# A sparse two-layer graph network: row variances and neighbour scores on ScalarE, Newton steps an iteration later, the last tiles' rows added singly, the stairs behind the projections

## The chip, the cores and the metric

The kernel runs on one core of a Trainium2 chip. A core has five engines that work side by side, each with a queue of its own that it works off in order: TensorE (PE, with its weight loads as PEld), VectorE (DVE), ScalarE (ACT), GpSimd (POOL) and SyncE (SP). Transfers between the chip's memory (DRAM) and the core's SBUF are done by 16 DMA engines; they are issued from the queues of SP, ACT or POOL. The metric is the time of one execution on the device in microseconds (us), lower is better.

## What is computed

x has 3327 rows of 512 numbers, adj is a sparse 0/1 matrix of 3327 by 3327 with ones on the diagonal. Two layers follow one another, each with a residual and a layer norm. In short:

```python
def layer0(X, A, W, b, a_self, a_neigh):           # 4 heads of 128
    feats  = einsum('nf,hfo->hno', X, W)
    logits = leaky(e_s[:, :, None] + e_n[:, None, :], 0.2)   # e_s, e_n: feats . a_self, feats . a_neigh
    attn   = softmax(logits - 1e10 * (1 - A))
    return relu(concat_heads(attn @ feats) + b)

def layer1(x, A, W_sa, a_sa, W_g, b_g, Wa, ba, Wb, bb):
    gate_a = sigmoid([A @ x, x] @ Wa.T + ba)       # one number a row
    gate_b = sigmoid([A @ x, x] @ Wb.T + bb)
    h      = x @ W_sa
    e      = where(A, exp(-leaky(s_left[:, None] + s_right[None, :], 0.01)), 0)
    x_a    = (e / (e.sum(1) + 1e-5)) @ h
    x_b    = A @ (x @ W_g) + b_g
    return sigmoid(gate_a * x_a + gate_b * x_b)

x = layernorm(x + layer0(x, adj, ...))
x = layernorm(x + layer1(x, adj, ...))
```

A row has few neighbours, so the kernel doesn't multiply by A: it finds for each row the list of its neighbours, and gathers their rows.

## The kernel before

**Tiles.** The 3328 padded rows are 26 tiles of 128, in two groups of 12 and 14. Within a group the rows are sorted by their number of neighbours, so that a tile j needs only `CAPS[j]` gathered rows for each of its own (14 down to 4). The first tile of each group (0 and 12) holds the few rows with more neighbours; what they have beyond `CAPS` comes by an extra gather, the **stairs**: `to_row`, `to_node` and `step_of` are small matrices that spread these extra entries onto rows of a tile and back. `climb` works out which rows the stairs gather (`ids2`) and their own scores (`es2`): two VectorE copies out of the sorted lists `srt`, a matmul with `to_row`, and four small VectorE operations.

**Stage 1.** For each tile, `features` (line 338 on) multiplies x by W on TensorE (16 matmul records at L346), copies the result with ACT into a `row` of 512 features and 8 scores (L350, L351), and POOL writes it into a table in DRAM, `table0` (L353). After the last tile, POOL also writes a very negative score into the table's one padding row, from `nrow` (L355). Between the projections, seven chunks of 512 columns of adj are turned into lists of neighbours: `make_codes` (matmuls on loads `at` that SP issues, 12 buffers for 13 loads a chunk), `turn_codes` (transposes, `pv`), and then `top_codes`, `decode` and `pick` on VectorE. A `rank` and a scatter through DRAM sort the rows (`sort`; lists are read back as `srt`), and POOL gathers the sorted x (`own_x`, L496). The loop that orders this by hand is:

```python
    for i in range(len(chunks)):
        make_codes(i)
        more(1)                      # features of one tile
        ...
        turn_codes(i); top_codes(i); decode(i); pick(i)
        ...
        if i == NC0 + 1:
            climb(0, ...)
        more(4)                      # features of up to four tiles
```

NC0 is 3, so `climb` for the first group stands in chunk 4, ahead of the last `more(4)`, which has the last two tiles left to project.

**Stage 2, layer 0.** POOL gathers rows one indirect DMA at a time (L602, 128 rows of 520 numbers each), three tiles ahead, into 7 buffers of 6 rows. For tile i the loop does in this order: gather for tile i+3; `publish` tiles whose statistics are finished (ACT scales and shifts the row, VectorE the 8 columns beside it, POOL scatters it into `table1`); `columns2` of tile i-2 (ACT copies the transposed rows out of PSUM, L757, TensorE multiplies them by 8 vectors, L760); `attend` tile i (two of three gathered rows are multiplied by their weights on VectorE, L733, the third on ACT, L731, and TensorE adds all of them up through an identity matrix, L736); tile i-1's residual y (L810), its transposes (`columns1`, L753) and its statistics (`norm.add`); `columns3` (L764); and the weights of tile i+1, with an exponential on ACT (`weigh_a`, L696 to L709, and `weigh_b`, L714 to L716).

**The norm.** `Norm.add` takes bn_stats and bn_aggr of each y on VectorE (L647, L648). When a group of up to four tiles is full, `rsqrt` follows at once: 13 small VectorE operations (L656 to L663), the core of them three Newton steps.

**Stage 3, layer 1.** The same gathers, from `table1`. `weights_a` adds the row's own score to the neighbours' on VectorE (L863), takes leaky (L870), the exponential on ACT (L872) and the gates; `weights_b` divides. `weighted` sums the rows times e on VectorE (L930), and for up to four or five pairs of rows (`paired`) also adds the two rows of a pair (L932), so that TensorE, which sums the rows unweighted (`plain_sum`, L951), has one matmul instead of two. `turn` and `project` transpose and multiply both sums by W_sa and W_g (L961, L970); then come the gated sum (L995), a tanh (L997), the residual (L1018), the norm and the scatter of the result (L1011, L143). The tiles' order in this layer is short ones first, then long and short in turn; the last four are 3, 17, 18 and 8, with 10, 9, 9 and 7 rows.

Of the kernel before, what the change touches and what calls it, by code (L numbers as in the profile page):

```python
# [8 lines left out]
F32 = mybir.dt.float32  # L9
AF = mybir.ActivationFunctionType  # L10
ALU = mybir.AluOpType
# [68 lines left out]
def sparse_pass(  # L80
# [212 lines left out]
    nc.gpsimd.dma_start(table1[N:NP, :], zrow)  # L293
    nrow = pj.tile([1, ROW], F32, name="nrow")
    nc.gpsimd.memset(nrow, 0.0)
    nc.gpsimd.memset(nrow[:, F : F + H], -BIG)

# [41 lines left out]
    def features(t):  # L339

        i = t * P // CH
        xc = xcs[i]
        o = t * P - chunks[i]
        pf = psf.tile([P, 2, 512], F32, tag="pf", name=f"pf{t}")
        for k, hh in ((k, hh) for hh in range(2) for k in range(KT)):
            nc.tensor.matmul(  # L346
                pf[:, hh, :HC], xc[:, k, o : o + P], w0[:, k, hh, :], start=(k == 0), stop=(k == KT - 1)
            )
        row = pj.tile([P, ROW], F32, tag="row", name=f"row{t}", bufs=4)
        nc.scalar.copy(row[:, 0:F].rearrange("p (h o) -> p h o", h=2), pf[:, :, 0 : F // 2])  # L350
        nc.scalar.copy(row[:, F:ROW].rearrange("p (h o) -> p h o", h=2), pf[:, :, F // 2 : HC])  # L351
        nc.scalar.copy(st[:, t, S + 2 : S + 2 + H].bitcast(F32), pf[:, 1, F // 2 : HC])  # L352
        nc.gpsimd.dma_start(table0[t * P : (t + 1) * P, :], row)  # L353
        if t == NT - 1:
            nc.gpsimd.dma_start(table0[N:NP, F : F + H], nrow[:, F : F + H])  # L355

# [193 lines left out]
    for i in range(len(chunks)):  # L550
# [9 lines left out]
        if i == NC0 - 1:  # L560
            rank_a(0)
        if i == NC0 + 1:
            climb(0, p0, psl.tile([P, CH], F32, tag="pc1", name="climb0")[:, : B + H])
        more(4)
    later(len(tasks))
    nc.sync.dma_start(own1[:, 0, :], xo)
    nc.sync.dma_start(own1[:, 1, :], table0[NG[0] * P : NP, :])
    rank_a(1)
    rankis[1] = rank_b(1)
# [74 lines left out]

    def stats(pool, y, mv):
        st6 = pool.tile([P, 6], F32, tag="st6", name=f"st6_{nc.next_id()}")
        nc.vector.bn_stats(st6, y)  # L647
        nc.vector.bn_aggr(mv, st6)  # L648

    def rsqrt(pool, mv, n, tag):  # L650

        v = pool.tile([P, GRP], F32, tag="rv", name=f"rv{tag}")[:, :n]
        r = pool.tile([P, GRP], F32, tag="rr", name=f"rr{tag}")[:, :n]
        t = pool.tile([P, GRP], F32, tag="rt", name=f"rt{tag}")[:, :n]
        d = pool.tile([P, GRP], F32, tag="rd", name=f"rd{tag}")[:, :n]
        nc.vector.tensor_scalar(v, mv[:, :n, 1], LN_EPS, None, ALU.add)  # L656
        nc.vector.tensor_scalar(t.bitcast(I32), v.bitcast(I32), 1, None, ALU.logical_shift_right)
        nc.vector.tensor_scalar(r.bitcast(I32), t.bitcast(I32), -1.0, float(0x5F3759DF), ALU.mult, ALU.add)
        for _ in range(3):
            nc.vector.tensor_mul(t, r, r)  # L660
            nc.vector.scalar_tensor_tensor(t, t, -0.5, v, ALU.mult, ALU.mult)
            nc.vector.scalar_tensor_tensor(r, t, 1.5, r, ALU.add, ALU.mult)
        nc.vector.scalar_tensor_tensor(d, mv[:, :n, 0], -1.0, r, ALU.mult, ALU.mult)  # L663
        return r, d

    class Norm:


        def __init__(self, pool, tag, ends):
            self.pool, self.tag, self.ends = pool, tag, ends  # L670
            self.first, self.mv = 0, None

        def add(self, k, y):

            if self.mv is None:
                self.mv = self.pool.tile([P, GRP, 2], F32, tag="mv", name=f"mv{self.tag}{k}")
            stats(self.pool, y, self.mv[:, k - self.first, :])
            if k not in self.ends:
                return None
            n = k - self.first + 1  # L680
            done = (self.first, *rsqrt(self.pool, self.mv, n, f"{self.tag}{k}"))
            self.first, self.mv = k + 1, None
            return done
# [66 lines left out]
    def columns1(j):  # L750
        pt = turned[j] = psx.tile([P, KT, P], F32, tag="pt", name=f"x1t{j}", bufs=2)
        for k in range(KT):
            nc.tensor.transpose(pt[:, k, :], row1(j)[:, k * P : (k + 1) * P], ident)  # L753

    def columns2(j):
        xt1 = m0.tile([P, KT, P], F32, tag="xt1", name=f"xt1_{j}")
        nc.scalar.copy(xt1, turned[j])  # L757
        pcol = psx.tile([P, B * H], F32, tag="pcol", name=f"pcol{j}", bufs=2)[:, :NCOL]
# [34 lines left out]
    weigh_b(order0[0])  # L793
    ready = [[], []]
    for i in range(NT + 3):
        if i + AHEAD < NT:
            j = order0[i + AHEAD]
            got[j] = gather(table0, j)
        for args in ready[0]:
            publish(*args)  # L800
        ready = [ready[1], []]
        if 2 <= i < NT + 2:
            columns2(order0[i - 2])
        if i < NT:
            attend(order0[i])
        if 0 < i <= NT:
            j = order0[i - 1]
            y = row1(j)[:, 0:F]
            xj = y if j < NG[0] else got[j][0][2][:, 0, 0:F]
            nc.vector.scalar_tensor_tensor(y, accs[j], 0.0, xj, ALU.max, ALU.add)  # L810
            columns1(j)
            done = norm.add(i - 1, y)
            if done:
                k0, scale, shift = done
                ready[1] = [
                    (order0[k], scale[:, k - k0 : k - k0 + 1], shift[:, k - k0 : k - k0 + 1]) for k in range(k0, i)
                ]
        if 2 <= i < NT + 2:
# [37 lines left out]
    def weights_a(j):  # L856

        c = slots(j)
        e = ew[j] = m1.tile([P, S + 1], F32, tag="e", name=f"e{j}", bufs=3)
        gate = gates[j] = m1.tile([P, 12], F32, tag="gate", name=f"gate{j}", bufs=5)  # L860
        nc.scalar.copy(e[:, 0:1], row1(j)[:, F + 6 : F + 7])
        for s0, n, g, _ in got[j]:
            nc.vector.tensor_scalar(e[:, s0 : s0 + n], g[:, :n, F], row1(j)[:, F + 3 : F + 4], None, ALU.add)  # L863
        if j in T0:
            small = ps1.tile([P, B * H], F32, tag="small", name=f"to_nodes1_{j}")
            cols = to_nodes(m1, small, f"l1_{j}", stair[j][:, F : F + 3])
            nc.vector.scalar_tensor_tensor(
                e[:, C0 + 1 :], cols[:, :, 0], row1(j)[:, F + 3 : F + 4], no_step, ALU.add, ALU.subtract
            )
# [30 lines left out]
    def paired(j):  # L900

        left = 4 + (CAPS[j] >= 13)
        got_ = set()
# [68 lines left out]
    ends = {3, 7, 11, 15, 19, 22, 24, 25}  # L972
    norm = Norm(m1, "n1", ends)
    at_ = lambda i: order[i] if 0 <= i < NT else None
# [4 lines left out]
    scaled_first(at_(0))  # L979
    ready = None  # L980
    for i in range(NT + 3):
# [11 lines left out]
        if jpp is not None:  # L993
            za = zs[jpp] = m1.tile([P, F], F32, tag="za", name=f"za{jpp}", bufs=GRP + 3)
            nc.vector.scalar_tensor_tensor(za, bias_g, gates[jpp][:, 1:2], proj[jpp], ALU.mult, ALU.add)  # L995

            nc.scalar.activation(za, za, AF.Tanh, scale=0.5)  # L997
        if jp is not None:
            project(jp, 0)
# [16 lines left out]
        if jpp is not None:  # L1016
            za = zs[jpp]
            nc.vector.scalar_tensor_tensor(za, za, 0.5, row1(jpp)[:, 0:F], ALU.mult, ALU.add)  # L1018
        if j1 is not None:
            weights_b(j1)  # L1020
            scaled_first(j1)
        if jpp is not None:
            ready = norm.add(i - 2, zs[jpp])

# [451 lines left out]
```

## Time and profile before

| what | value |
|---|---|
| time, three runs | 1015.5, 1017.0, 1017.8 us |
| the profiled run | 1008.2 us, span 1006.5 us |
| PE busy | 798.0 us, 79% |
| DVE busy | 719.3 us, 71% |
| POOL busy | 635.8 us, 63% |
| ACT busy | 270.5 us, 27% |
| DMA | 221.9 MB, 220 GB/s on average |

A profile is one execution. Busy times are sums over the engine's own instructions, so an engine that waits for another shows as idle; the time between two instructions of a queue ("issue") isn't counted as busy either. The stages lie one behind the other: up to about 197 us projections and lists, to 593 us layer 0, then layer 1. Since their limits differ, an engine's share of the whole span says little: one asks in each stage which wait ends last.

### The profile page before, as it was taken

What the parts mean: (1) busy time and instruction counts of PE and PEld (TensorE: products, weight loads), DVE (VectorE), ACT (ScalarE), POOL (GpSimd) and SP (SyncE); (2) the same over time, 40 slices, a digit from 0 to 9 for tenths busy, and PEclk for the clock granted to TensorE, in tenths of its full rate; (3) what the DMA queues carried; (4) which work ended last, traced back from release to release, by engine and by line L of the source; (5) the groups of instructions that cost most, each with busy time, mean ns of one, the idle gap of its engine ahead of it and who ended that gap; (6) DMA issues with size and microseconds to landing.
All of it is one profiled execution on the core that took longest, in us unless ns stands there. A gap on an engine that the chain in (4) does not pass through costs nothing.

```text
span 1006.5 us, 9964 instructions
## 1 busy us (share of the span) xinstructions
PE 798.0 (79%) x2534; PEld 422.2 (42%) x2534; DVE 719.3 (71%) x2131; ACT 270.5 (27%) x737; POOL 635.8 (63%) x677
## 2 busy tenths in 40 slices
PE   4398982518797996989698949998998989898991
PEld 3277762204344443444344424444444434343440
DVE  4277896586366673856566848897987989899882
ACT  1021210103134242333424413323221232321331
POOL 6611151577777777777777647777777777777211
PEclk9699995657889998889899968999999999999996
DMA  8799995995877777777777537776776667767200
GB/s 321 291 356 400 367 388 197 322 372 200 269 206 206 219 207 225 209 232 229 218 237 230 178 118 199 192 193 197 192 194 194 177 185 189 199 184 190 72 32 34
DMA packets 71954, 221.86 MB, mean 220 GB/s; under 512 B 13425, under 2 KB 17697, under 8 KB 70993
## 3 DMA queue, kind: packets, MB, share of 16 engines
q0 software_dynamic: 48000, 157.07, 52.7%
q1 hardware_dynamic: 22784, 61.97, 16.3%
q10 hardware_dynamic: 1104, 2.10, 0.6%
q8 instruction: 23, 0.38, 0.1%
q14 instruction: 43, 0.34, 0.1%
HBM read 200.01 MB, written 28.54 MB: 227 GB/s over the span
## 4 chain that ended last, share of the span: by engine, by line
PE 31%; DMA 17%; POOL 17%; DVE 16%; issue 13%; ACT 4%; DVEq 0%; POOLq 0%; ACTq 0%
POOL g L602 12%; PE acc L736 12%; DMA g<-table,srt 12%; PE pf L346 8%; DVE sw L930 6%; PE po L970 3%; DVE g L932 2%; PE pcol L760 2%; DMA at<-in_adjB 2%; PE acc L725 2%; PE acc L951 2%; ACT za L1011 1%; POOL out L143 1%; DMA a_row<-in_a_self 1%; POOL sprod L316 1%
## 5 line engine op out<-in xcount | busy, mean ns | idle before, releaser
L602 POOL DMA_INDIRECT g<-table,srt x464 | 477.2, 1028 | 145.8 <-issue 126.0
L736 PE MATMUL acc<-g,ident 128*128 128x512 f32 x504 | 232.5, 618 | 1.5 <-DVE g L733 1.5
L930 DVE SCALAR_TENSOR_TENSOR sw<-g,e,sw 128x512 f32<-128x512 f32 x226 | 169.3, 749 | 15.8 <-ACT sw L914 11.7
L736 PEld LDWEIGHTS acc<-g,ident 128*128 128x128 f32 x504 | 101.2, 201 | 133.6 <-issue 105.9
L951 PE MATMUL acc<-g,ident 128*128 128x512 f32 x262 | 124.9, 606 | 19.7 <-DVE g L932 19.6
L346 PE MATMUL pf<-w,xc 128*128 128x260 f32 x416 | 100.1, 402 | 13.8 <-DVE w L289 13.8
L733 DVE TENSOR_TENSOR g<-g,w 128x512 f32<-128x512 f32 x176 | 110.5, 695 | 0.6
L970 PE MATMUL po<-wsa,sT 128*128 128x512 f32 x208 | 95.6, 603 | 0.2 <-ACT sT L963 0.2
L346 PEld LDWEIGHTS pf<-w,xc 128*128 128x128 f32 x416 | 82.5, 201 | 28.6 <-DVE w L289 14.3
L970 PE MATMUL po<-wg,sT 128*128 128x512 f32 x208 | 93.5, 593 | 0.0
L731 ACT ACTIVATE g<-g,w 128x128 f32<-128x128 f32 x304 | 91.6, 390 | 2.7 <-DVE w L716 2.7
L951 PEld LDWEIGHTS acc<-g,ident 128*128 128x128 f32 x262 | 49.1, 192 | 88.4 <-issue 44.2
L353 POOL DMA_DIRECT2D table<-row x26 | 14.4, 554 | 95.2 <-ACT st L352 81.2
L932 DVE TENSOR_TENSOR g<-g 128x512 f32<-128x512 f32 x95 | 65.7, 691 | 3.3
L696 DVE TENSOR_TENSOR w<-g,srt 128x20 f32<-128x20 f32 (+3 forms) x55 | 9.7, 180 | 80.7 <-DMA g<-table,srt 79.7
L760 PE MATMUL pcol<-v,xt 128*128 128x8 f32 x208 | 33.2, 287 | 40.5 <-ACT xt L757 40.5
L143 POOL DMA_INDIRECT out<-za,srt x26 | 28.3, 1090 | 54.7 <-ACT za L1011 48.6
L970 PEld LDWEIGHTS po<-wsa,sT 128*128 128x128 f32 x208 | 40.6, 195 | 51.7 <-issue 49.5
L997 ACT ACTIVATE za<-za 128x512 f32<-128x512 f32 x26 | 16.4, 632 | 167.0 <-DVE za L995 167.0
L970 PEld LDWEIGHTS po<-wg,sT 128*128 128x128 f32 x208 | 39.6, 190 | 49.7 <-issue 49.2
L709 ACT ACTIVATE w<-w 128x40 f32<-128x40 f32 (+10 forms) x26 | 6.2, 237 | 176.8 <-DVE w L708 176.8
L760 PEld LDWEIGHTS pcol<-v,xt 128*128 128x128 f32 x208 | 30.9, 228 | 46.0 <-ACT xt L757 46.0
(234 smaller groups left out, 954.5 us busy)
## 6 DMA issues: line engine op xcount, KB each, us to landing
at<-in_adjB SPq DMA_DIRECT2D x78, 512.0 KB, 11.7
g<-table,srt POOLq DMA_INDIRECT x464, 3.8
table<-row POOLq DMA_DIRECT2D x26, 260.0 KB, 5.8
xc<-in_xB SPq DMA_DIRECT2D x6, 1024.0 KB, 7.4
own<-in_xo SPq DMA_DIRECT2D x1, 3640.0 KB, 31.2
own<-table SPq DMA_DIRECT2D x1, 3640.0 KB, 49.6
at<-in_adjL SPq DMA_DIRECT2D x13, 256.0 KB, 7.3
w<-in_W0B SPq DMA_DIRECT2D x1, 1040.0 KB, 6.9
```

Of the source, the lines that this page charges most:

```text
L143: put = nc.gpsimd.indirect_dma_start(out=dst, out_offset=bass.IndirectOffsetOnAxis(ap=rows, axis=0), in_=src, in_offset=None, bounds_check ...
L346: nc.tensor.matmul(pf[:, hh, :HC], xc[:, k, o : o + P], w0[:, k, hh, :], start=(k == 0), stop=(k == KT - 1))
L602: nc.gpsimd.indirect_dma_start(out=buf[:, q - q0, :], out_offset=None, in_=table[:, :], in_offset=bass.IndirectOffsetOnAxis(ap=srt[g][:, i ...
L725: nc.tensor.matmul(acc, ident, bias0, start=True, stop=False)
L731: nc.scalar.activation(gv[:, h, :], gv[:, h, :], AF.Copy, scale=w[:, s, h : h + 1])
L733: nc.vector.tensor_tensor(gv, gv, w[:, s, :].rearrange("p (h o) -> p h o", o=1).to_broadcast([P, H, FO]), ALU.mult)
L736: nc.tensor.matmul(acc, ident, buf[:, o + s - s0, 0:F], start=False, stop=(s == CAPS[j] and j not in T0))
L760: nc.tensor.matmul(pcol, xt1[:, k, :], v1[:, k, :], start=(k == 0), stop=(k == KT - 1))
L930: nc.vector.scalar_tensor_tensor(sw, g[:, i, 0:F], e[:, s : s + 1], sw, ALU.mult, ALU.add)
L932: nc.vector.tensor_add(g[:, i, 0:F], g[:, i - 1, 0:F], g[:, i, 0:F])
L951: nc.tensor.matmul(plain[j], to, row, start=(not sums_of_two and i == 0), stop=(sums_of_two and i == len(rows) - 1),)
L970: nc.tensor.matmul(proj[j], sT[:, k, :], wt[:, k, :], start=(half + k == 0), stop=(half + k == KT))
```

## The change

1. **Variances.** bn_stats and bn_aggr go. The VectorE operation that makes y (L810, and L1018 in layer 1) also puts out its row sum; one small VectorE operation makes minus the mean of it, and ACT squares y with that as its bias and puts out the sum of squares (`AF.Square` with `accum_out`).
2. **Newton steps.** `rsqrt` becomes `Norm.finish` and is called one iteration after the group's last `add`: in layer 0 behind `attend`, in layer 1 behind the tanh. The published tiles and the iteration that uses the result stay.
3. **Scores.** In layer 1 the sums of scores (L863) are made by ACT (`AF.Identity` with a bias).
4. **Columns.** In layer 0 the copy out of PSUM moves from the head of `columns2` to the end of `columns1`, so one iteration's part of ACT's queue now has it ahead of the exponential of the next tile, and `columns2` itself comes behind `attend`.
5. **Unpaired rows.** For the last four tiles of layer 1 at most one pair of rows is added up on VectorE.
6. **Stairs.** `climb(0, ...)` moves from chunk 4 to behind the loop over the chunks, ahead of the second group's ranks.
7. **Padding row.** Its score isn't written by a DMA of its own; ACT's copy of the last tile's scores has a bias `pad` that is very negative in that row. `nrow` and its transfer go.

```diff
+    pad = p0.tile([P, 1], F32, name="pad")
+    nc.gpsimd.memset(pad, 0.0)
+    nc.gpsimd.affine_select(pad, pad, ..., fill=-BIG, base=P - 2, channel_multiplier=-1)
...
-        nc.scalar.copy(row[:, F:ROW]..., pf[:, :, F // 2 : HC])
+        nc.scalar.activation(row[:, F:ROW]..., pf[:, :, F // 2 : HC], AF.Identity,
+            bias=pad if t == NT - 1 else 0.0)
...
-        if t == NT - 1:
-            nc.gpsimd.dma_start(table0[N:NP, F : F + H], nrow[:, F : F + H])
...
-        if i == NC0 + 1:
-            climb(0, p0, psl.tile(...)[:, : B + H])
         more(4)
     later(len(tasks))
     nc.sync.dma_start(own1[:, 0, :], xo)
     nc.sync.dma_start(own1[:, 1, :], table0[NG[0] * P : NP, :])
+    climb(0, p0, psl.tile(...)[:, : B + H])
     rank_a(1)
...
-    def stats(pool, y, mv):
-        nc.vector.bn_stats(st6, y)
-        nc.vector.bn_aggr(mv, st6)
...
         def add(self, k, y):
+            nc.vector.tensor_scalar(less_mean, less_mean, -1.0 / F, None, ALU.mult)
+            nc.scalar.activation(square, y, AF.Square, bias=less_mean, accum_out=self.of[:, 1, i : i + 1])
+            return k in self.ends
+        def finish(self, k):               # what rsqrt did
...
     def columns1(j):
         ...
             nc.tensor.transpose(pt[:, k, :], row1(j)[:, k * P : (k + 1) * P], ident)
+        xt1s[j] = m0.tile([P, KT, P], F32, tag="xt1", name=f"xt1_{j}")
+        nc.scalar.copy(xt1s[j], pt)
     def columns2(j):
-        nc.scalar.copy(xt1, turned[j])
...
+        if i < NT:
+            attend(order0[i])
         if 2 <= i < NT + 2:
             columns2(order0[i - 2])
-        if i < NT:
-            attend(order0[i])
+        if full:
+            k0, scale, shift = norm.finish(i - 2)
...
-            nc.vector.scalar_tensor_tensor(y, accs[j], 0.0, xj, ALU.max, ALU.add)
+            nc.vector.scalar_tensor_tensor(y, accs[j], 0.0, xj, ALU.max, ALU.add, accum_out=norm.total(i - 1))
...
-            nc.vector.tensor_scalar(e[:, s0 : s0 + n], g[:, :n, F], row1(j)[:, F + 3 : F + 4], None, ALU.add)
+            nc.scalar.activation(e[:, s0 : s0 + n], g[:, :n, F], AF.Identity, bias=s_left)
...
-        left = 4 + (CAPS[j] >= 13)
+        left = 4 + (CAPS[j] >= 13) if j not in order[-4:] else 1
...
+        if full:
+            ready = norm.finish(i - 3)     # layer 1, behind the tanh
...
-            nc.vector.scalar_tensor_tensor(za, za, 0.5, row1(jpp)[:, 0:F], ALU.mult, ALU.add)
+            nc.vector.scalar_tensor_tensor(
+                za, za, 0.5, row1(jpp)[:, 0:F], ALU.mult, ALU.add, accum_out=norm.total(i - 2))
```

## The prediction

> **What bounds the kernel now.** I read the page first (span 1006.5 us; POOL 63%, DVE 71%, PE 79% busy, none of them near full), then the three stages one by one, because the mean hides that each has its own limit.
>
> Stage 1 (0 to 197 us: projections `features`, neighbour codes). The timeline around 150 to 200 us shows it:
>
> ```profile
> 148.10 0.95 PE L393 MATMUL pv<-ident,v 128*128 128x128 f32 x8
> ...
> 169.38 0.58 PE L538 MATMUL climb<-of,to_row 128*128 128x14 f32 x2 [20.32 <-DVE of L537]
> ...
> 169.79 8.89 PE L346 MATMUL pf<-w,xc 128*128 128x260 f32 x32
> ...
> 176.21 0.60 POOL L353 DMA_DIRECT2D table<-row  x1 [13.97 <-ACT row L351]
> ...
> 186.91 0.40 DVE L72 MAX8 ent<-pv 128x8 f32<-128x224 f32 x1 [16.29 <-PE pv L393]
> ...
> 187.31 0.57 POOL L355 DMA_DIRECT2D table<-nrow  x1 [6.11 <-DMA table<-row]
> ...
> 197.05 1.01 POOL L602 DMA_INDIRECT g<-table,srt  x1 [0.30 <-issue]
> ```
>
> (Columns of a timeline: start and length in us, engine, line, operation, count, and in brackets the idle time before it with what ended it.) TensorE stands 20.3 us before the stairs' small matmul, because its input is a VectorE copy queued behind chunk 4's codes. The last two projections wait behind it, so ACT, the row writes on POOL (14 us) and chunk 5's codes on VectorE (16.3 us) are late in turn; then POOL waits 6.1 us more to write `nrow`.
>
> Stage 2 (197 to 593, layer 0). POOL issues the gathers; its waits and the others' in that stretch:
>
> ```profile
> POOL g L602 <- issue: 60.5, 191, 2.6
> ...
> POOL table L143 <- ACT x1b L768: 5.3, 1, 5.3
> ```
>
> ```profile
> DVE w L696 <- DMA g<-table,srt: 79.2, 21, 8.6
> ...
> PE pcol L760 <- ACT xt L757: 40.5, 24, 7.5
> ```
>
> POOL's "issue" gaps are 0.3 us each between gathers of 0.95: one each 1.257 us without a break to 569 us, while VectorE waits 79 us for rows. So POOL is the bound up to the last tiles, and TensorE's 40.5 us of waiting for the turned rows' copy is mostly free. At the end it isn't; the timeline of the last tiles:
>
> ```profile
> 566.93 0.60 PE L753 MATMUL x1t<-ident,x1b 128*128 128x128 f32 x4
> ...
> 568.26 1.06 PE L760 MATMUL pcol<-v,xt 128*128 128x8 f32 x8 [0.73 <-ACT xt L757]
> ...
> 569.17 1.11 PE L725 MATMUL acc<-bias,ident 128*128 128x512 f32 x2
> ...
> 570.12 5.31 PE L736 MATMUL acc<-g,ident 128*128 128x512 f32 x12
> ...
> 572.25 0.22 ACT L709 ACTIVATE w<-w 128x20 f32<-128x20 f32 x1 [1.70 <-DVE w L708]
> ```
>
> TensorE runs without a break, 3.2 us from one tile's last accumulation (566.93) to the next one's first (570.12), and the following tile's exponential (572.25) is done in the middle of the accumulation.
>
> Stage 3 (593 to 1006, layer 1), stage table, columns us, PE, PEld, DVE, ACT, POOL busy (counts), clock:
>
> ```profile
> 600.00:700.00 100.00, 89.26 (x245) 42.38 (x246) 82.08 (x207) 31.10 (x77) 77.75 (x74) 0.94 0.70 198
> 700.00:932.00 232.00, 215.47 (x573) 100.39 (x572) 209.51 (x490) 61.32 (x145) 179.60 (x166) 0.97 0.68 189
> 932.00:985.00 53.00, 49.16 (x136) 22.48 (x134) 43.29 (x108) 17.35 (x35) 8.04 (x8) 1.00 0.13 45
> ```
>
> From 700 on the chain runs along VectorE, op after op with 0.02 us between; TensorE idles only 16.5 of 232 us and 3.8 of the 53 after the last gather. Two engines are nearly full, so relief of one is capped by the other.
>
> [...] an accumulator output is a second instruction; on ACT the trace shows it (0.19 us, behind L872), on VectorE nothing before has one. [...]
>
> **The change, part by part.**
>
> *Stairs moved, `nrow` replaced.* The one `climb` (2 copies, a matmul, 4 small ops) goes from inside chunk 4 to behind chunk 6; no DMA goes with it. TensorE then goes at 149.1 to the last 32 matmuls (8.9 us) and at 158 to chunk 5's codes. Twelve of its 13 loads are there by about 164 (DMA share 0.94 to 164, then under 0.1 until 176); the 13th follows the first use, 4 to 6 us. So chunk 5's codes are ready near 168, and VectorE, free at 169, goes on: 186.9-169 = 18, less about 2 us for `climb`, now on its path: **16 us** earlier. POOL is free at 160.0 (`srt` lands). It has 12 row gathers at 1.257 and two writes at 0.9, 17 us, and begins the layer-0 gathers at 177 instead of 197.05: **20 us**. The last row write is issued near 168 and lands 6.4 us later, in time. The `nrow` write (0.6 and a 6.1 us wait) is in that sum; its substitute is two POOL memsets in idle time and a bias on an ACT copy of 8 columns, nothing. `ids2` is first needed by POOL 28 gathers later (177+35 = 212); `climb` is done at about 205. Ranks of the second group, queued behind `climb` on VectorE, come at 211, the list scatters need them at 213.5: just in time.
>
> *Layer 0, order.* `columns2` moves behind `attend`: TensorE no longer waits for the copy ahead of its accumulation. But the copy xt1 and the new Square now stand on ACT **ahead of the next tile's exponential**, and the copy waits for a transpose that TensorE does after the whole current accumulation. So in a TensorE-bound tile the gap becomes: pcol 0.91, transposes 0.55, copy 0.1+0.58, Square 0.72+0.19, exponential 0.28, three small VectorE ops 0.65, first multiply 0.7, hop 0.1 = 4.8 us, against 3.2: **+1.6 us a tile**. Where POOL binds it is hidden: POOL needs 1.257 a row and 1.3 a scatter, TensorE 0.86 a row, so 4.8-1.3 = 3.5 is covered from 3.5/0.4, about 9 rows. All but the small tiles have that; the last five or six don't. bn_stats and bn_aggr (0.9) leave VectorE, where there was slack.
>
> Layer 0's end: the last gather ends at 563.6, lands at 567.3; with sum, maximum, exponential, division and first multiply it could start 2.7 us later (the same ops around 572 us) and accumulate in 4.3, so end at 574.3; it ended at 582.7, so TensorE was 8.4 behind. After: 574.3-20 = 554.3, plus 8.4, plus 1.6 x 5 to 6 = 571. The 20 us shrink to **-11.5**. The closing chain has Square for bn_stats, +0.5.
>
> *Layer 1.* VectorE loses bn_stats+bn_aggr (0.90 a tile) and the score sums (49 ops, 0.33 a tile), gains a small op (0.17) and perhaps a readback (0 to 0.2; I take 0.15): -0.9 a tile. [...] ACT gains 0.91 and 0.35 a tile at 27% load: hidden, but VectorE's L870 now waits some 0.4 us for it in tiles with no second part. Over the 16 tiles of 700 to 932 that offers 14 us, TensorE allows at most 16.5 and keeps its waits for scaled rows and stairs: I take -8, and -2 before 700. POOL's last gather now has 23 us before its tile begins, so it doesn't bind. The Newton steps move without new cost (they wait one iteration, used at the same point).
>
> *Unpaired rows of the last four tiles* (10, 9, 9, 7 rows): 11 adds at 0.69 leave VectorE (7.6 us), 11 matmuls at 0.86 come to TensorE (9.5 us). There TensorE had about 5.5 us idle over the four: **+4**. Bounds: -3 (VectorE decides to the end) to +9.5.
>
> Sum: -11.5+0.5-8-2+4 = **-17 us** on the profile's 1006.5. That run took 1008.2; the three timed ones 1015.5 to 1017.8, so I scale: 1017.0 x 989.5/1006.5 = **1000 us**.
>
> **Rivals.**
> 1. *Both gains arrive whole* (24%): layer 0's end keeps 20, since ACT's queue drains while POOL still delivers, and layer 1 gives 14. For: TensorE's lag of 8.4 came partly from the copy. Against: the order of ACT's queue. -35: 981 us.
> 2. *Accumulation and unpaired rows eat layer 1* (17%): [...] the tail costs 9; layer 1 is +3. For: [...] TensorE at 93%. [...] -8: 1009 us.
> 3. *Slower* (6%): the ACT queue decides in every tile. Layer 0 has 254 rows, 218 us on TensorE; it starts at 213 (the first multiply is at 229.8 now, less 16), seven publications add 12. It ends where it did (583) if the gap is (583-213-12-218)/26 = 5.4 us; with layer 1's 6 from 5.6 on the kernel is slower. At 6.2 it is +15: 1032 us. Against: 4.8 is summed from measured pieces.
> 4. *No net change* (3%): the 13th load or the row write comes late, the stairs bring 8 us, and 2 happens too.
>
> **From this the numbers.** Forecast 50%, own range 991 to 1008. Two runs of 0.2% (2 us) apart can't be told from no change. Faster: 0.49+0.24+0.16 = 0.89; same 0.04; slower 0.07. For 8 in 10 the range takes half of rival 1 and nearly all of 2: 981 to 1013.
>
> **What would show it.** Right: first layer-0 gather near 177; no 20 us wait ahead of `climb`; in the last layer-0 tiles exponentials directly behind Square, gap 4.8; TensorE the chain's engine in layer 1. Wrong: [...] POOL waiting for ranks near 213; chunk 5's codes later than 172; a closing stretch after the last gather not longer than before.

## The result and the profile after

| kernel | median us | runs |
|---|---|---|
| before | 1016.26 | 1013.59 to 1017.82 |
| changed | 1026.91 | 1024.4 to 1028.95 |

The changed kernel is slower: ratio 1.0106, 95% interval 1.007 to 1.0143. The forecast was 1000 us, faster. The profiled run has a span of 1027.2 us against 1006.5 of before, so the profiles differ by 20.7 us, and that sum is what is taken apart here. The profiled run of before is a quick one (1008.2 us; its timed runs took 1013.6 to 1017.8) and that of the changed kernel the slowest of its four, so about half of the 20.7 us is spread between runs.

On the page, VectorE's busy time fell as meant (719.3 to 670.1 us) and ScalarE's rose (270.5 to 318.3). The chain that ended last says where to look:

```profile
PE 40%; DVE 18%; issue 15%; POOL 11%; DMA 9%; ACT 5%; DVEq 0%; ACTq 0%; POOLq 0%
PE acc L740 19%; PE po L980 9%; PE acc L961 8%; DMA g<-table,srt 6%; DVE sw L940 6%; POOL g L605 5%; DVE g L942 2%; DVE g L737 2%; PE pt L971 1%; ACT squaren L668 1%; DMA table<-row 1%; ACT za L1023 1%; POOL table L359 1%; PE pcol L768 1%; DMA a_row<-in_a_self 1%
```

Layer 0's accumulation (L740) now holds 19% of the chain; before, the same matmuls (then L736) held 12%, as much as the gathers, and POOL and DMA together 34%.

**Stage 1 did what was forecast.** The timeline of the changed kernel, same columns as in the prediction:

```profile
151.16 7.20 PE L349 MATMUL pf<-w,xc 128*128 128x260 f32 x32
...
171.43 0.40 DVE L72 MAX8 ent<-pv 128x8 f32<-128x224 f32 x1
...
179.57 0.95 POOL L605 DMA_INDIRECT g<-table,srt  x1 [0.30 <-issue]
```

The last projections run at once, chunk 5's codes start on VectorE at 171.43 instead of 186.91 without a wait, and POOL's first layer-0 gather is issued at 179.57 instead of 197.05, 17.5 us earlier.

**Layer 0 gave it all back.** Waits of the changed kernel from 212 to 594 us (columns: engine and line, what it waited for, us in total, times, longest):

```profile
ACT xt L760 <- PE x1t L757: 211.3, 25, 12.7
...
DVE x1a L772 <- PE pcol L768: 79.6, 12, 9.5
...
PE acc L740 <- DVE g L737: 59.9, 22, 6.5
...
DVE x1b L772 <- PE pcol L768: 56.9, 12, 7.2
...
DVE w L700 <- DMA g<-table,srt: 5.0, 3, 4.1
```

VectorE no longer waits for gathered rows (5.0 us; 79.2 before): the rows are there and it comes late. It waits 136.5 us for `pcol`, the 8 columns that TensorE now makes behind the whole accumulation, and TensorE in turn waits 59.9 us for multiplied rows, where before the same wait (at L736) was 1.5. One tile shows the circle (timeline, TensorE, VectorE and ScalarE):

```profile
518.61 0.48 PE L768 MATMUL pcol<-v,xt 128*128 128x8 f32 x3
518.94 0.63 PE L757 MATMUL x1t<-ident,x1b 128*128 128x128 f32 x4
519.13 0.17 DVE L772 COPY x1b<-pcol 128x8 f32<-128x8 f32 x1 [5.02 <-PE pcol L768]
519.30 0.41 DVE L700 TENSOR_TENSOR w<-g,srt 128x16 f32<-128x16 f32 x2
...
519.61 0.59 ACT L760 COPY xt<-x1t 128x512 f32<-128x512 f32 x1 [6.44 <-PE x1t L757]
...
520.10 0.72 ACT L668 ACTIVATE squaren<-x1b,ofn 128x512 bf16<-128x512 f32 x1
...
520.81 0.22 ACT L713 ACTIVATE w<-w 128x36 f32<-128x36 f32 x1
...
521.76 3.70 DVE L737 TENSOR_TENSOR g<-g,w 128x512 f32<-128x512 f32 x6
522.50 9.69 PE L740 MATMUL acc<-g,ident 128*128 128x512 f32 x18 [2.06 <-DVE g L737]
```

VectorE's first operation for the next tile (L700) stands behind the copy of `pcol`, which stands behind the accumulation; ScalarE's exponential (L713) stands behind the copy of the turned rows and Square, which stand behind the same accumulation. Before, the next tile's exponential ran in the middle of it. From the end of one accumulation to the first matmul of the next it is 4.2 us in plain tiles and 5.7 us in tiles with publications; before it was 3.0 where the rows were there.

**And the accumulations themselves became slower.** The weight loads of the tile above, one by one:

```profile
523.47 0.19 PEld L740 LDWEIGHTS acc<-g,ident 128*128 128x128 f32 x1 [0.18 <-issue]
524.13 0.34 PEld L740 LDWEIGHTS acc<-g,ident 128*128 128x128 f32 x1 [0.47 <-issue]
524.98 0.34 PEld L740 LDWEIGHTS acc<-g,ident 128*128 128x128 f32 x1 [0.52 <-issue]
...
526.69 0.34 PEld L740 LDWEIGHTS acc<-g,ident 128*128 128x128 f32 x1 [0.52 <-issue]
527.31 0.19 PEld L740 LDWEIGHTS acc<-g,ident 128*128 128x128 f32 x1 [0.28 <-issue]
527.74 0.19 PEld L740 LDWEIGHTS acc<-g,ident 128*128 128x128 f32 x1 [0.24 <-issue]
```

Here a load takes 0.34 us instead of 0.19, and the next one follows after 0.85 us instead of 0.43, with nothing waited for: TensorE runs at half rate for some 3 us, about 1 us after it resumed. Of the 504 loads of layer 0's accumulations 66 took over 0.3 us, against 35 before. The page has 251.2 us for all these matmuls against 232.5 before, for the same work.

The trace also records the clock that TensorE was granted (columns: stretch and its length in us, then PE, PEld, DVE, ACT and POOL busy with counts, the granted clock, the DMA share, GB/s):

```profile
506.58:510.00 3.42, 1.66 (x9) 0.83 (x8) 2.15 (x10) 1.86 (x6) 2.69 (x3) 1.00 0.83 197
510.00:513.41 3.41, 3.10 (x7) 1.43 (x8) 3.41 (x7) 3.17 (x11) 2.50 (x4) 1.00 0.84 282
...
520.23:523.65 3.42, 1.36 (x4) 0.67 (x4) 2.68 (x8) 2.69 (x10) 2.51 (x4) 1.00 0.57 221
523.65:527.06 3.41, 3.41 (x5) 1.35 (x5) 2.57 (x6) 1.72 (x6) 2.80 (x3) 0.50 0.54 156
```

All 50 stretches of this record begin on a grid of 3.413 us. The same pause of 2.1 us stands ahead of two tiles that follow each other. The first pause (508.2 to 510.3) is cut by the grid at 510.00: TensorE was busy for 1.66 us of the stretch before, and the clock stays at full (1.00). The second (520.4 to 522.5) lies inside one stretch: TensorE was busy for 1.36 us of it, 40%, and the next stretch is granted at half (0.50). In layer 0 of this kernel, 14 of the 15 switches to half follow a stretch in which TensorE was busy for 40% or less, the 15th one with 75%; wherever the clock stayed at full it was 45% or more. The clock isn't at half much longer than before (68.0 us between the first and the last accumulation; 58.7 before), but the half now falls on accumulations, for 57.1 us against 23.7. An estimate from these two: half of the difference, 16.7 us, is lost, of the 18.7 us by which they grew.

**Layer 1.** VectorE's waits in it, the largest rows, changed kernel:

```profile
DVE sw L940 <- ACT sw L924: 26.4, 24, 2.4
DVE e L880 <- ACT e L873: 21.0, 12, 9.5
DVE za L1005 <- PE po L980: 20.5, 5, 6.0
```

and kernel before:

```profile
DVE sw L930 <- ACT sw L914: 11.7, 12, 1.7
...
DVE e L870 <- ACT e L861: 6.2, 10, 1.3
DVE za L995 <- PE po L970: 3.6, 2, 2.0
```

VectorE has some 30 us less to do there and waits some 46 us more in these three rows; 9.9 us of it stood before as a wait for gathered rows at the score sums (L863), which ScalarE has now.

### The profile page after: what moved, and what is told of

Same layout as the page of the kernel before. It is cut to its first block, busy times and chain, and to the rows that moved or that the text cites. A ratio compares the mean times of both kernels' runs of the same rounds, so it can differ in the third digit from the quotient of the medians.

```text
span 1027.2 us, 10168 instructions
## 1 busy us (share of the span) xinstructions
PE 820.5 (80%) x2556; PEld 427.8 (42%) x2556; DVE 670.1 (65%) x2071; ACT 318.3 (31%) x890; POOL 638.4 (62%) x676
## 4 chain that ended last, share of the span: by engine, by line
PE 40%; DVE 18%; issue 15%; POOL 11%; DMA 9%; ACT 5%; DVEq 0%; ACTq 0%; POOLq 0%
PE acc L740 19%; PE po L980 9%; PE acc L961 8%; DMA g<-table,srt 6%; DVE sw L940 6%; POOL g L605 5%; DVE g L942 2%; DVE g L737 2%; PE pt L971 1%; ACT squaren L668 1%; DMA table<-row 1%; ACT za L1023 1%; POOL table L359 1%; PE pcol L768 1%; DMA a_row<-in_a_self 1%
## 5 line engine op out<-in xcount | busy, mean ns | idle before, releaser
L740 PE MATMUL acc<-g,ident 128*128 128x512 f32 x504 | 251.2, 658 | 62.1 <-DVE g L737 59.9
L740 PEld LDWEIGHTS acc<-g,ident 128*128 128x128 f32 x504 | 104.3, 211 | 210.6 <-issue 101.8
L940 DVE SCALAR_TENSOR_TENSOR sw<-g,e,sw 128x512 f32<-128x512 f32 x226 | 169.4, 750 | 30.9 <-ACT sw L924 26.4
L961 PE MATMUL acc<-g,ident 128*128 128x512 f32 x284 | 133.0, 604 | 12.4 <-DVE g L942 12.3
L349 PE MATMUL pf<-w,xc 128*128 128x260 f32 x416 | 104.0, 413 | 13.3 <-DVE w L289 13.3
L349 PEld LDWEIGHTS pf<-w,xc 128*128 128x128 f32 x416 | 84.9, 207 | 29.9 <-DVE w L289 14.1
L961 PEld LDWEIGHTS acc<-g,ident 128*128 128x128 f32 x284 | 54.3, 193 | 84.6 <-issue 56.8
L760 ACT COPY xt<-x1t 128x512 f32<-128x512 f32 x26 | 15.2, 586 | 215.0 <-PE x1t L757 215.0
L942 DVE TENSOR_TENSOR g<-g 128x512 f32<-128x512 f32 x84 | 58.1, 691 | 2.9
L377 PE MATMUL pc<-at,pow 128*32 128x512 bf16 (+1 forms) x182 | 23.8, 432 | 32.4 <-DMA at<-in_adjB 18.6
L353 ACT COPY row<-pf 128x512 f32<-128x512 f32 x26 | 15.3, 587 | 98.4 <-issue 55.0
## 6 DMA issues: line engine op xcount, KB each, us to landing
at<-in_adjB SPq DMA_DIRECT2D x78, 512.0 KB, 11.5
```

The costliest lines, as they stand in the source:

```text
L349: nc.tensor.matmul(pf[:, hh, :HC], xc[:, k, o : o + P], w0[:, k, hh, :], start=(k == 0), stop=(k == KT - 1))
L377: nc.tensor.matmul(pc[32 * c : 32 * c + 32, : nt * P], pow2[:, s, :], loaded[i, m], start=(s == 0), stop=(m + 1 not in ms or s == 3),)
L740: nc.tensor.matmul(acc, ident, buf[:, o + s - s0, 0:F], start=False, stop=(s == CAPS[j] and j not in T0))
L940: nc.vector.scalar_tensor_tensor(sw, g[:, i, 0:F], e[:, s : s + 1], sw, ALU.mult, ALU.add)
L942: nc.vector.tensor_add(g[:, i, 0:F], g[:, i - 1, 0:F], g[:, i, 0:F])
L961: nc.tensor.matmul(plain[j], to, row, start=(not sums_of_two and i == 0), stop=(sums_of_two and i == len(rows) - 1),)
```

## The experiments

Ratios are to the kernel before, run beside each on the same chip (its medians were 1013.8 to 1015.3 us, and 1016.3 beside the changed kernel, so medians of different sets can be compared to about 2 us).

| kernel | median us | ratio | 95% interval |
|---|---|---|---|
| e1 stairs alone | 994.04 | 0.9801 | 0.9756 to 0.9846 |
| e2 changed, columns' copy late | 1027.51 | 1.0140 | 1.0101 to 1.0180 |
| e3 changed, ScalarE's copy and Square late | 1017.39 | 1.0036 | 1.0018 to 1.0055 |
| e4 changed, both late | 1003.94 | 0.9905 | 0.9873 to 0.9937 |
| e5 changed, more TensorE work | 1012.03 | 0.9975 | 0.9961 to 0.9989 |
| e6 = e1 + layer 1's relief | 994.68 | 0.9815 | 0.9778 to 0.9852 |
| e8 = e4 with the pairs | 1001.64 | 0.9873 | 0.9843 to 0.9902 |
| e9 = e1 less one row a tile | 976.91 | 0.9619 | 0.9590 to 0.9648 |
| e10 = e6, publications late | 996.26 | 0.9810 | 0.9788 to 0.9832 |
| e11 = e10, residual late too | 988.68 | 0.9749 | 0.9729 to 0.9769 |
| e12 = e1, publications late | 992.85 | 0.9775 | 0.9755 to 0.9796 |
| e13 = e8 in e11's order | 997.01 | 0.9844 | 0.9817 to 0.9871 |

### e1: what the stairs alone bring

```diff
 # kernel before, and of the change only:
-        if i == NC0 + 1:
-            climb(0, ...)
+    climb(0, ...)            # behind the loop over the chunks
-    nrow ... and its transfer
+    pad ..., bias=pad if t == NT - 1 else 0.0
```

> The kernel before with nothing but the stairs moved behind the chunks and the padding row's score by ACT's bias. Theory: GpSimd's row of gathers, 0.3 us apart from the first of layer 0 to the last of layer 1, is what sets the time of the kernel before in both layers; it starts some 17.5 us earlier, as it did in the changed kernel, so the whole run is 16 to 18 us shorter: about 999 us. Rival (a step of the prediction): the end of layer 0 hangs on TensorE, and only 11.5 us of it arrive: about 1005 us. Second rival: the earlier start is lost in the first tiles, which wait for ranks and list scatters: within 3 us of before.

994.04 us, a gain of 1.99%, 20 us. Profile against profile it is 12.4 us (span 994.1 against 1006.5; the profiled run of before took 1008.2 us, less than the others of that table). POOL's first gather comes at 181.66, 15.4 us earlier, and layer 0's last accumulation ends at 570.71 instead of 582.91, 12.2 earlier. The large part of the change that helps is this one. The prediction put 20 us on the stairs by themselves; its -11.5 is what was left of them after the cost of layer 0's order, which e1 doesn't have. By medians these 20 us arrive whole, by the profiles 12 of them.

### e2, e3, e4: which of the two queues

```diff
 # e2
-        if 2 <= i < NT + 2:
-            columns3(order0[i - 2])
         if i + 1 < NT:
             weigh_a(order0[i + 1]); weigh_b(order0[i + 1])
+        if 2 <= i < NT + 2:
+            columns3(order0[i - 2])
 # e3
     def columns1(j): ... transposes
-        nc.scalar.copy(xt1s[j], pt)
-            full = norm.add(i - 1, y)
         ...
             weigh_a(order0[i + 1]); weigh_b(order0[i + 1])
+        if 0 < i <= NT:
+            nc.scalar.copy(xt1s[j], turned[j])       # j = order0[i - 1]
+            full = norm.add(i - 1, row1(j)[:, 0:F])
 # e4: both
```

> The changed kernel, with the VectorE copy of the 8 columns behind the next tile's weights instead of ahead of them. Theory (two queues, each enough by itself): ScalarE's exponential still stands behind the copy of the turned rows and Square, both behind TensorE's whole accumulation, so the gap between two accumulations stays at 4.2 us: 1024 to 1028 us. Rival (VectorE's queue alone is the cause): the gap falls to 3 us or less and the time to about 1004 us. Rival (the sums and squares themselves cost it): no change, and none in the next two kernels either.

> The changed kernel, with the copy of the turned rows, the small VectorE operation and Square behind the next tile's exponential; the VectorE copy of the columns stays where it is. Theory (two queues): VectorE's weights of the next tile still stand behind a copy that waits for the whole accumulation; the exponential comes only 0.4 us earlier a tile, so 5 to 10 us are won: about 1018 us. Rival (ScalarE's queue alone decides, the prediction's third rival): the gap falls to 3 us and the time to about 1004 us.

> Both moves of the two kernels before this one. Theory (two queues): the next tile's weights are worked out during the accumulation again, the gap falls to about 2.6 us (columns, transposes, bias), GpSimd is the bound again and keeps its start of 17.5 us; layer 1 stays at nothing, the unpaired last tiles cost 5: 1003 to 1006 us. Rival (the sums, squares and slow clock themselves are the cause): over 1018 us.

e2 changes nothing: the gap stays at 4.2 us, and layer 0's last accumulation ends at 593.5 (591.2 in the changed kernel). e3 brings 10 us, its plain gaps are about 3.9 us and 51 loads take over 0.3 us; the last accumulation ends at 581.0. Together they bring 23 us, and it ends at 566.0. TensorE's timeline of e4:

```profile
503.99 0.95 PE L769 MATMUL pcol<-v,xt 128*128 128x8 f32 x8
504.80 0.63 PE L757 MATMUL x1t<-ident,x1b 128*128 128x128 f32 x4
505.27 1.02 PE L729 MATMUL acc<-bias,ident 128*128 128x512 f32 x2
506.13 8.13 PE L740 MATMUL acc<-g,ident 128*128 128x512 f32 x18
514.10 0.95 PE L769 MATMUL pcol<-v,xt 128*128 128x8 f32 x8
```

No bracket, so no wait: the gap is 2.1 us, shorter than in the kernel before, and the 9.69 us of the same tile are 8.13. Either queue alone kept the next tile's weights behind the accumulation; in the changed kernel the exponential starts 0 to 0.65 us after VectorE has its input ready, so the two delays end nearly together, and lifting one only shows the other. The sums and squares are still made in e4, on the same engines: it was their place, not their work.

### e5: more work on TensorE

```diff
+        for _ in range(2):
+            nc.tensor.matmul(acc, ident, bias0, start=True, stop=True)
         nc.tensor.matmul(acc, ident, bias0, start=True, stop=False)
```

> The changed kernel, with the bias matmul at the head of each layer-0 accumulation done three times instead of once (the first two results are overwritten, so the sums are the same; it is 2 us more TensorE work a tile, about as long as TensorE stands idle there). Theory (clock): part of the slower accumulations, 251 us against 232 before, is TensorE at half rate after each idle gap of 2.1 us; filled gaps leave fewer than 30 half-rate weight loads in layer 0 instead of 60, and the kernel with more work is 5 to 10 us faster than the changed one: 1017 to 1022 us. Rival (the slow matmuls wait for their multiplied rows): as many of them, 1027 us, or up to 10 us slower where the extra work lies on the path.

1012.03 us: the changed kernel with two superfluous matmuls a tile takes 15 us less than without them (1026.9; 13 us by the ratios). Its timeline (TensorE, then weight loads):

```profile
523.56 1.88 PE L730 MATMUL acc<-bias,ident 128*128 128x512 f32 x4
525.28 1.02 PE L731 MATMUL acc<-bias,ident 128*128 128x512 f32 x2
526.64 7.13 PE L742 MATMUL acc<-g,ident 128*128 128x512 f32 x16 [0.34 <-DVE g L739]
```

```profile
527.60 0.19 PEld L742 LDWEIGHTS acc<-g,ident 128*128 128x128 f32 x1 [0.18 <-issue]
528.03 0.19 PEld L742 LDWEIGHTS acc<-g,ident 128*128 128x128 f32 x1 [0.24 <-issue]
528.46 0.19 PEld L742 LDWEIGHTS acc<-g,ident 128*128 128x128 f32 x1 [0.24 <-issue]
```

The gap between accumulations is still 4.2 us (522.4 to 526.6), but TensorE stands idle for only 0.34 us of it, and the loads behind it run at full rate (0.19 us). Loads over 0.3 us in layer 0 fall from 66 to 23 (the expectation has 60 for the 66), the accumulations from 251.2 to 231.8 us, and the last one ends at 578.1 instead of 591.2. The rows come no sooner, so the slow matmuls were not slow because they waited for rows. It was expected to be 5 to 10 us; it was more.

The two granted clocks, 1.00 and 0.50, go with the two lengths of a load, 0.19 and 0.34 us. Each of the 16 returns to full in layer 0 of the changed kernel follows a stretch of 3.413 us in which TensorE was busy for at least 92%. The half doesn't take an idle stretch: 40% busy stood ahead of it at 523.65. Of the two pauses of 2.1 us shown above, the one that falls into one stretch was followed by the half, and the one that the grid cuts wasn't; about half of the tiles were hit (15 switches to half over 26 tiles). That the busy share of the stretch decides is the author's reading of these coincidences; e5 shows that filling the pauses takes most of the half-rate loads away (66 to 23).

### e6 and e9: what sets layer 1

```diff
 # e6: e1, and in layer 1 only
+            nc.scalar.activation(e[:, s0 : s0 + n], g[:, :n, F], AF.Identity, bias=...)
+            ... accum_out=norm.total(i - 2); Square on ScalarE; finish behind the tanh
 # e9: e1, with slot 3 of every tile left out of the weighted sum
-                nc.vector.scalar_tensor_tensor(sw, g[:, i, 0:F], e[:, s : s + 1], sw, ...)
+                if s != 3:
+                    nc.vector.scalar_tensor_tensor(sw, g[:, i, 0:F], e[:, s : s + 1], sw, ...)
```

> The kernel of the stairs alone, with layer 1's variances and score sums on ScalarE and its Newton steps one iteration later, as in the change (layer 0 and the pairs as before). Theory: GpSimd sets layer 1 up to its last gather, so VectorE's relief of 0.9 us a tile gives nothing before and at most 3 tiles' worth after it: the same as the stairs alone, within 3 us (991 to 997 us). Rival (the prediction's step: VectorE sets layer 1): 8 to 10 us faster, about 985 us.

> The kernel of the stairs alone, leaving out one weighted row (slot 3) of every tile in layer 1: 26 VectorE operations of 0.75 us, 19 us less on VectorE, all gathers kept. Theory (GpSimd sets layer 1 up to its last gather): only the tiles behind the last gather get shorter, 0 to 3 us: 991 to 994 us. Rival (VectorE sets layer 1): 15 to 19 us faster, 975 to 979 us.

The theory on record here, that GpSimd sets layer 1, fell. It got the first kernel right (994.68, nothing gained) and the second wrong: e9 is 17 us faster than e1 by medians, and in the profiles layer 1 takes 398.5 us instead of 413.1, 14.6 less for some 18 us less of VectorE's work there. So VectorE's row of work does set layer 1, as the prediction said, and yet 23 us of relief in e6 (VectorE busy 341.0 to 318.0 us over layer 1) bring nothing. From layer 1's first gather to the end of the span it is 413.1 us in e1 and 417.3 in e6.

The lines of VectorE between two tiles' weighted sums show why. Kernel before (e1 has the same order), timeline of VectorE:

```profile
784.42 0.29 DVE L895 TENSOR_SCALAR e<-e,gate 128x9 f32<-128x9 f32 x1
784.62 0.69 DVE L647 BATCH_NORM_STATS2 st<-za 128x6 f32<-128x512 f32 x1
785.34 0.18 DVE L648 BATCH_NORM_AGGREGATE mvn<-st 128x2 f32<-128x6 f32 x1
785.50 1.54 DVE L930 SCALAR_TENSOR_TENSOR sw<-g,e,sw 128x512 f32<-128x512 f32 x2
```

and changed kernel:

```profile
797.41 0.51 DVE L905 TENSOR_SCALAR e<-e,gate 128x9 f32<-128x9 f32 x1
797.62 0.30 DVE L666 TENSOR_SCALAR ofn<-ofn 128x1 f32<-128x1 f32 x1
798.71 1.54 DVE L940 SCALAR_TENSOR_TENSOR sw<-g,e,sw 128x512 f32<-128x512 f32 x2 [0.79 <-ACT sw L924]
```

The first weighted row is made by ScalarE (0.72 us) from the weights that VectorE has just finished (L895, L905), and VectorE goes on with it. bn_stats and bn_aggr, 0.87 us, lay exactly in that time. Taken away, they leave a wait of 0.73 to 0.79 us in most tiles, up to 2.4 where rows are published. In e6's layer 1 the wait for ScalarE's `sw` is 26.4 us (11.7 in e1) and the wait for its scores, or for the rows behind them, 23.9 (16.4 in e1, of which 10.1 is put down to the DMA). The relief turned into waits of its own size.

### e10, e11, e12: filling that shadow

```diff
 # e10 (on e6) and e12 (on e1): order in an iteration of layer 1
-  weights_a | scale finished rows, scatter | residual | weights_b, scaled_first
+  weights_a | residual | weights_b, scaled_first | scale finished rows, scatter
 # e11 (on e6)
+  weights_a | weights_b, scaled_first | scale finished rows, scatter | residual
```

> The kernel with the stairs and layer 1's variances and scores on ScalarE, with the scaling of finished rows on ScalarE (four of 0.72 us) moved behind the first scaled row of the next tile instead of ahead of it. Theory (shadow): VectorE sets layer 1, but the operations that the change took off it stood in the shadow of its wait for ScalarE's first scaled row, which now shows as 0.73 us in every tile and 2.4 us in the six tiles with publications; 1.7 us of these six go: 8 to 10 us faster, 985 to 987 us. Rival (GpSimd or TensorE sets layer 1 and VectorE's waits are free): 993 to 996 us as before the move.

> As the last, with VectorE's residual (0.69 us and its readback) also moved behind the first scaled row, where it fills the remaining 0.73 us of waiting; in exchange the division of the next tile's weights waits for ScalarE's gates, 0.3 to 0.5 us a tile. Theory (shadow): 5 to 10 us faster than the last, 976 to 982 us. Rival (the wait for the gates takes it all back): the same as the last, 985 to 987 us. Second rival (waits are free): 993 to 996 us.

> The kernel of the stairs alone (layer 1's variances and scores on VectorE as before), with the same move of the scaling behind the first scaled row. Theory (shadow): its wait of 1.7 us in six tiles goes as well, 7 to 10 us faster than the stairs alone: 985 to 987 us, the same as with the relief of VectorE; the relief is then worth nothing in either order. Rival (the relief counts once the publications are out of the way): the first kernel of these three is 5 us or more faster than this one.

e10 missed: 996.26 us where 985 to 987 was expected. Its wait for `sw` did fall, from 26.4 to 18.2 us, but the wait of the stairs' tiles for TensorE (`to_nodes`) rose from 9.3 to 16.3 and that for the projections from 7.3 to 9.7. Why TensorE is late just there isn't settled. e11 gained 7.6 us on e10, about what was expected of that step: the wait for `sw` is 2.4 us, and the residual (0.69 us) now does what bn_stats did. From layer 1's first gather to the end e11 takes 410.1 us, e12 411.9 and e1 413.1. e12 gained 0.3% on e1, less than half of what was expected and well within the intervals. Of the two kernels with this order, the one with the relief (e10, 0.9810) isn't faster than the one without (e12, 0.9775), so the last rival fell: the relief is worth nothing in either of these two orders. e11's order without the relief wasn't run.

### e8 and e13: the pairs, and the change put in order

```diff
 # e8 = e4, and
-        left = 4 + (CAPS[j] >= 13) if j not in order[-4:] else 1
+        left = 4 + (CAPS[j] >= 13)
 # e13 = e8 with e11's order in layer 1
```

> The changed kernel with both ScalarE's and VectorE's late pieces behind the next tile's weights, and with the pairs of the last four tiles as before. Theory: unpairing costs 4 to 5 us of TensorE in the stretch after the last gather, so this is 4 to 5 us faster than the same kernel unpaired: 999 to 1000 us. Rival (VectorE decides to the end): 3 us slower than unpaired, 1007 us.

> Everything that the change has but the unpaired rows, each piece in the order that the other kernels pointed to: both late pieces of layer 0 behind the next tile's weights, and in layer 1 the first scaled row ahead of the scaling of finished rows and of VectorE's residual. Theory: layer 1 gains 6 to 8 us against the same kernel without the second reordering (1001.6 us): 994 to 996 us, which is still slower than the kernel that has layer 0 as before and the same layer 1 (988.7 us), because layer 0's squares cost 3 to 6 us. Rival (layer 0's squares cost nothing once they are placed behind): 988 to 990 us.

e8 is 2.3 us below e4, with intervals that overlap; the profiles say 3.4 us (417.3 against 420.7 from the first gather of layer 1 to the end; the five kernels with this layer 1 and unpaired rows have 420.0 to 420.9). Unpairing the last rows costs that. e13, 997.01 us, is slower than e11 by 8 us, which differs from it in layer 0 only; from layer 1's first gather on both take 410 us. In the profiles it is 1.6 us: e13's accumulations end 3.7 us earlier (566.0 against 569.7), and its closing, shown in the next section, takes 5.2 us more. The profiles are of runs of 993.9 us (e13) and 992.1 (e11), so they don't show where the 8 us between the medians come from. That layer 0's new norm gains nothing even when placed well is what both say. The best kernel here is e11, with layer 0 as before, the stairs moved, and layer 1's relief in another order: 0.9749. How much of its 3 us in layer 1 is the relief and how much the order stays open.

## Why the prediction was wrong

The profiles' 20.7 us, put together from the runs, beside the steps of the prediction:

| step | forecast | measured | from |
|---|---|---|---|
| stairs and layer 0's order, up to the last accumulation | -20 + 8.5 = -11.5 | -12.2 + 20.5 = +8.3 | 582.91 to 570.71 (e1) to 591.24 (changed) |
| closing of layer 0 | +0.5 | +5.3 | last accumulation to layer 1's first gather, 10.3 to 15.6 |
| layer 1's relief | -10 | +4.2 | 413.1 (e1) to 417.3 (e6) |
| unpaired rows | +4 | +3.1 | 417.3 (e6) to 420.4 (changed) |
| sum | -17 | +20.9 | |

**Stairs: right.** POOL's start moved by 17.5 us for 20 forecast, VectorE's codes by 15.5 for 16. How much of that reaches the end of layer 0 is the least certain number of the table: e1's last accumulation is the latest of six kernels with the same layer 0 and stairs (566.6 to 570.7), and from before to e1 it is 12.4 us in the profiles but 20 in the medians. From e1 to the changed kernel both say 33 us, so the losses below don't hang on the run of before.

**Layer 0's order: the step that failed.** The gap itself was summed well: 4.8 us forecast against 3.2, so +1.6; measured 4.2 against 3.0, +1.2. What failed is the next sentence, "where POOL binds it is hidden", from about 9 rows on. It reckoned TensorE at 0.86 us a row, full rate, behind every gap (its third rival has 218 us for all rows; they took 232.5 even before). But idle gaps were followed by half rate (0.50 granted) in about half of the tiles (+18.7 us in the accumulations, 251.2), and publications make the gap 5.7 us, not 4.8. With both, TensorE was slower than POOL in nearly all tiles, not in the last five or six: the order cost 20.5 us where 8.5 was forecast. Beginning 13.8 us earlier, it took 3.4 us more in gaps (short ones grew; the long waits for POOL shrank) and 18.7 more in accumulations: 8.3 us later at the end. The prediction also saw only ScalarE's queue; that the copy of `pcol` holds VectorE's weights behind the same accumulation it missed. e2 to e4 show that mending what it did see would have brought 10 us of 23. Its third rival named this outcome, but only from a gap of 5.4 to 5.6 us on in every tile, publications counted apart; plain gaps were 4.2, and the clock did the rest.

**Closing: mis-sized.** "The Newton steps move without new cost" holds inside the layer, not at its end. The changed kernel's last tile:

```profile
593.89 0.15 DVE L677 TENSOR_SCALAR rvn<-ofn 128x1 f32<-128x1 f32 x1 [1.26 <-ACT squaren L668]
...
596.22 0.16 DVE L684 TENSOR_TENSOR rdn<-ofn,rrn 128x1 f32<-128x1 f32 x1
596.29 0.68 DVE L824 SCALAR_TENSOR_TENSOR x1b<-acc,g 128x512 f32<-128x512 f32 x1
```

The last accumulation was done at 591.24, but its residual (L824) is queued behind the Newton steps of the tile before, which wait for Square, and begins at 596.29. Each of the seven kernels with layer 0's new norm has 15.6 us there, also where the columns are mended (e4, e8, e13), and each of the seven with the old one 10.2 to 10.5. So it comes with the change in layer 0; that it is the place of the Newton steps was read in the traces and not tried by itself.

**Layer 1: right bound, wrong relief.** The step took VectorE's operations off its chain at their full length, 0.9 us a tile. e9 shows that work on that chain does count (14.6 of some 18 us). But these operations stood beside a wait for ScalarE, and what was seen as hidden in the other direction ("VectorE's L870 now waits some 0.4 us") was the smaller of the new waits. Forecast -10, measured +4.2.

**Unpaired rows:** forecast +4, measured +3.1.

The accumulating residual (L1030) has its old length (0.685 us for 0.684) and so is no cause; of the signs named ahead, POOL waiting for ranks near 213 didn't happen. The sign that would have told the failure, TensorE's rate behind a gap, was not on the list.

## What to carry to other kernels

When an operation is moved in a queue, ask for every engine what the next tile's first operation stands behind: here two queues each put it behind a whole accumulation, and mending one alone showed nothing (e2) or less than half (e3). An operation that sits where its engine would wait anyway can cost nothing, and taking it away bring nothing (e6: 23 us less work on VectorE in layer 1, 994.68 us against 994.04); look at what comes next on that engine, and whether it has an input that isn't ready yet. A pause of TensorE can cost more than its length: here, with pauses of 2.1 us, the matmuls behind them became slower as well (251.2 us for all of layer 0's accumulations, 232.5 before).

## What the runs showed of the hardware

- In layer 0 of the changed kernel, with pauses of 2.1 us on TensorE and 4.2 us from accumulation to accumulation, the granted clock fell to half (0.50) 15 times over the 26 tiles, 11 times for 3.4 us and four times for 6.8, in the tile shown from 1.1 us after TensorE resumed. Which tiles were hit went with where the pause fell on a grid of 3.413 us: stretches with TensorE busy for 40% or less were followed by the half, stretches with 45% or more left it at full, with one exception (75%). The line wasn't sharp: behind this layer a stretch with 49% (from 591.92) was followed by the half, and in the kernel before one with 42% (from 545.17) was not. Two superfluous matmuls of about 1 us in each gap made the kernel 13 to 15 us faster (e5).
- A VectorE operation with a row sum as a second output kept its length: L1030 takes 0.685 us for 512 elements from two SBUF sources, as L1018 did without it (0.684), and 0.082 us follow to read the sum out.
